# Halving the 512-column float32r products of a linear-attention and feed-forward layer, with their order and their weights' addresses changed

## The chip, the cores and the metric

The kernel runs on one core of a Trainium2 chip. The metric is device time in microseconds of one launch, as the median of several runs. Five engines matter: TensorE (PE in the profile; its weight loads are PEld), VectorE (DVE), ScalarE (ACT), GpSimd (POOL) and SyncE (SP), which issues the loads and stores.

## What is computed

One layer on `x` of 4 x 2048 tokens with 256 features, all in float32: a linear attention in chunks of 32 tokens, a residual and a layer norm, then a gated feed-forward part of 768 hidden features whose weights are integers, a residual and a layer norm. Cut to what matters:

```python
Q, K, V = x @ W_q.T, x @ W_k.T, x @ W_v.T
S = einsum('bncd,bnkd->bnck', Qc, Kc) * mask          # chunks of 32, causal, decayed
O = einsum('bnck,bnkd->bncd', S, Vc).reshape(B, T, D)
attn = sigmoid(x @ W_g.T) * O @ W_o.T + x
x = layernorm(x + attn)
h = silu(x @ (w_gate * SCALE).T) * (x @ (w_up * SCALE).T)
x = layernorm(x + h @ (w_down * SCALE).T)
```

## The kernel before

The 8192 tokens are cut into 16 blocks of 512 (`TB`), with features or tokens on the 128 partitions. The code is written out block by block in Python, so each engine's instructions follow in the order of the program text: `in_turn` keeps an instruction in that order, and nearly all of them are kept so. Each engine then works through its own queue and waits there for what the next instruction needs. A steady block of the trace mixes the stages of three token blocks: the feed-forward part of block b, the out projection of block n = b + 2, and the y, v and gate products of block m = b + 3.

Precision is kept by splitting operands. A float32 operand of the attention projections is split into a high and a low float32r part, and a third one called gap; a product then consists of three: high, low, and gap. `pieces_of_tokens` (L464) makes the parts of the tokens: `high` on ACT (x_hi, go_hi, L472), `low` on POOL (L476), `difference` on DVE (x_gap, go_gap, L481). `three` (L535) makes the products: for each of two PSUM banks the high and low products on TensorE and then a scaling of the bank in place on ACT (L542); its returned function `others` adds the gap products and then calls `finish` for each bank. `feature_major` (L495) has the weights of the layer as stationary operand and 512 columns of tokens moving: y (p_y) and the gate (p_g), L501. `token_major` (L513) has the tokens stationary and 256 columns moving: v (p_v) and the out projection (p_o), L523.

The feed-forward part splits into a float32r high and a float16 low part instead. `ffn_up` (L912) makes one of six hidden chunks hc: two high and two low products into the gate's bank (fg), as many into the up bank (fu), 512 columns each (L923), the high ones ahead for an even hc and the low ones for an odd one, then silu on ACT (s, L932). Its `multiply` makes u on DVE (L943), u_hi on ACT (L948) and u_lo on POOL (L949), at once or, when held, where the caller asks for it. `project_back_late` (L755) multiplies u with the down weights (fdn, L764, 256 columns): `high` and then `low`. `ffn_down` (L966) adds the residual on DVE (L982) and its moments.

The loop from L1157 sets the order. A steady block (b of at least 1, m below 16) issues: normalization of h on ACT, up 0, up 1, transposes of h on DVE (`move_h`, L867), y, the rest of up 1, up 2, y's third products with the yT copies on DVE (L567), up 3, scores (ps, L663), values (po, L699) and goT on DVE (L718), up 4, the parts of goT, v, gate, v's third products with two copies of v on ACT (L576), the gate's third with two tanh on ACT (L559), x_hi of the first half, up 5, x_hi of the second half and x_gap of the first, u of chunk 5, x_gap of the second half, out (`split_out`, L824), `split_h` (hT_hi on ACT, hT_lo on POOL, L899 and L900), the first two fdn chunks, out's third products, with the residual h on DVE (L832) and its moments, x_lo on POOL, the root on ACT, the other fdn chunks, high and then low, with minus_h, scale_h and shift_h on DVE (L388, L389) ahead of the ffn residual. Blocks with b of 1 to 11 cut the tokens of a later block (m + 1 below 16); b = 12 does not. The last two blocks have an order of their own.

PSUM has eight banks, taken in turn by `bank` (L118): a bank is free again when what was in it eight requests ago has been read. The tiles that live through the whole kernel, all weights and their parts among them, lie in one pool, `const`.

The function that a float32r product of 512 columns comes from, and the start of the steady order after the values:

```python
def feature_major(a, b):
    def product(i, pb, kind):
        for k in range(KD):
            in_turn(nc.tensor.matmul(pb, lhsT=a[kind][:, k, i * P : (i + 1) * P],
                                     rhs=b[kind][:, k, :], start=kind + k == 0,
                                     stop=True, skip_group_check=True))
    return product
```

Of the kernel before, what the change touches and what calls it, by code (L numbers as in the profile page):

```python
# [47 lines left out]
F32 = mybir.dt.float32  # L48
# [6 lines left out]
P = 128  # L55
# [21 lines left out]
def kernel(  # L77
# [21 lines left out]
    assert NB > 3  # L99

    const = ctx.enter_context(tc.tile_pool(name="const", bufs=1))
    setup = ctx.enter_context(tc.tile_pool(name="setup", bufs=2))
    xin = ctx.enter_context(tc.tile_pool(name="xin", bufs=2))
    work = ctx.enter_context(tc.tile_pool(name="work", bufs=2))
# [9 lines left out]

    def in_turn(ins):
        tc.keep_in_program_order(ins)

    def bank(name):  # L118
        return psum.tile([P, TB], F32, tag="ps", name=name)
# [22 lines left out]

    def load_w(eng, w, name, pieces=1):
        k, n = w.shape[0] // P, w.shape[1]
        t = const.tile([P, k, n], w.dtype, tag=name, name=name)
        per = k // pieces
        for i in range(0, k, per):
            eng.dma_start(
                t[:, i : i + per, :], w.rearrange("(k p) n -> p k n", p=P)[:, i : i + per, :]
            )  # L150
        return t
# [58 lines left out]
    nc.vector.memset(half, -0.5)  # L210


    m_sb = const.tile([P, KD, D], F32, tag="m", name="m_sb")

    def make_m():
        pm = bank("pm")
# [12 lines left out]

    diff = const.tile([P, CHUNK], I32, tag="diff", name="diff")
    for g in range(P // CHUNK):
        nc.gpsimd.iota(
            diff[g * CHUNK : (g + 1) * CHUNK, :],
# [1 line left out]
            base=0,  # L237
            channel_multiplier=-1,
        )
    chunk_mask = const.tile([P, CHUNK], F32, tag="chunk_mask", name="chunk_mask")  # L240
    nc.vector.tensor_scalar(chunk_mask, diff, 0.0, None, ALU.is_ge)
    table = tiny.tile([P, 1], F32, tag="table", name="table")
    in_turn(nc.scalar.activation(table, eps, AF.Sigmoid))
# [32 lines left out]
    def integers(w, w_int, name):  # L276

        k, n = w.shape[0] // P, w.shape[1]
        both = [
            const.tile([P, k, n], dtype, tag=f"{name}_{kind}", name=f"{name}_{kind}")  # L280
            for kind, dtype in (("hi", F32R), ("lo", F16))
        ]
# [20 lines left out]

    def wide_counter():

        wide = const.tile([P, top.shape[1]], F32, tag="wide", name="wide")
# [135 lines left out]
    def weight_parts(w, name, tags):  # L442

        hi, lo = (
            const.tile([P, KD, D], F32R, tag=tag, name=f"{name}_{kind}")
            for tag, kind in zip(tags, ("hi", "lo"))
        )
# [9 lines left out]
    def weight_gap(name):  # L457

        hi, lo = w_parts[name]
        gap = const.tile([P, KD, D], F32R, tag=name, name=f"{name}_gap")  # L460
# [27 lines left out]
    def token_parts(t, name):  # L488
# [3 lines left out]
            low(k)  # L492
        return parts, lambda: [difference(k) for k in range(KD)]

    def feature_major(a, b):  # L495


        def product(i, pb, kind):
            for k in range(KD):
                in_turn(  # L500
                    nc.tensor.matmul(  # L501
                        pb,
                        lhsT=a[kind][:, k, i * P : (i + 1) * P],
                        rhs=b[kind][:, k, :],
                        start=kind + k == 0,
                        stop=True,
                        skip_group_check=True,
                    )
                )

        return product

# [396 lines left out]
        while late_splits:  # L909
            late_splits.pop(0)()  # L910

    def ffn_up(b, hT, uT, chunks, cols=slice(0, TB), held=False, low_first=False):  # L912

        n = cols.stop - cols.start
        for hc in chunks:
            pg = bank(f"fg_{b}_{hc}_{cols.start}")[:, :n]
            pu = bank(f"fu_{b}_{hc}_{cols.start}")[:, :n]

            kinds = (1, 0) if hc % 2 or low_first else (0, 1)
            for kind in kinds:  # L920
                for pb, w in ((pg, fg), (pu, fu)):
                    for dc in range(KD):
                        product = nc.tensor.matmul(  # L923
                            pb,
                            lhsT=w[kind][:, dc, hc * P : (hc + 1) * P],
                            rhs=hT[kind][:, dc, cols],
                            start=(kind == kinds[0] and dc == 0),
                            stop=(kind == kinds[1] and dc == KD - 1),
                        )
                        in_turn(product)  # L930
            s = work.tile([P, n], F32, tag="s", name=f"s_{b}_{hc}")
            in_turn(nc.scalar.activation(s, pg, AF.Silu, scale=SCALE / H_UP))  # L932
# [7 lines left out]
            def multiply(hc=hc, pu=pu, s=s):  # L940
                u = work.tile([P, n], F32, tag="u", bufs=3, name=f"u_{b}_{hc}")
                in_steady_turn(
                    nc.vector.scalar_tensor_tensor(u, pu, U_UP / H_UP, s, ALU.mult, ALU.mult)  # L943
                )
                hi, lo = uT[0][hc][:, cols], uT[1][hc][:, cols]

                def split():
                    in_steady_turn(nc.scalar.copy(hi, u))  # L948
                    in_steady_turn(nc.gpsimd.tensor_tensor(lo, u, hi.bitcast(F32), ALU.subtract))  # L949

                if lagging:
                    late_splits.append(split)
                else:
                    split()

            if held:
                return multiply
            multiply()
# [198 lines left out]
    for b in range(NB - 2):  # L1157
# [8 lines left out]
        sT, v, sg = ahead  # L1166
        if not more:
            scales_next = iterated_scale_and_shift(mv_out, of_out, f"out_{b}")
        if b:
            normalize(hs[b + 1], *scales_h)  # L1170
            up_now(b, hT, uT, 0)
        multiply = ffn_up(b, hT, uT, range(1, 2), held=True)
        if b:
            moving = move_h(b + 1, hs[b + 1])
        else:
# [19 lines left out]
            moving = move_h(b + 1, hs[b + 1])  # L1195
        if not more:
            go_parts, go_gaps = token_parts(goT, f"go_{n}")
        multiply = ffn_up(b, hT, uT, range(3, 4), held=True)
        if b > 1:
            normalize(r_before, *scales_out, range(NG // 2, NG))  # L1200
        multiply()
# [2 lines left out]
        if more:  # L1204
            sT_next = attn_scores(m, yT)
            goT = attn_values(n, sT, v, sg)
            multiply = ffn_up(b, hT, uT, range(4, 5), held=True, low_first=True)
            go_parts, go_gaps = token_parts(goT, f"go_{n}")
            if b == 0:
                cast_fd(1, range(1))  # L1210
            multiply()
            go_gaps()
            v_next, v_rest = split_v(m, x_parts)
            sg_next, g_rest = split_gate(m, x_parts)
            v_rest()
            late = b > 0
            if late:
                g_rest()
                if m + 1 < NB:
                    x_parts, x_high, x_low, x_difference = pieces_of_tokens(  # L1220
                        xTs[m + 1], f"x_{m + 1}"
                    )
                    x_high(0)
                multiply = ffn_up(b, hT, uT, range(5, 6), held=True)
                if m + 1 < NB:
                    x_high(1)
                    x_difference(0)
                multiply()
                if m + 1 < NB:
                    x_difference(1)  # L1230
            else:
                if b == 0:
                    cast_fd(1, range(1, 2))
                up_with_cast(b, hT, uT, 5, 1, range(2, 3))
        else:
            up_now(b, hT, uT, 4)
# [349 lines left out]
    with tc.If(wide_any > 0, preferred_fallthrough_block=False):  # L1586
# [15 lines left out]
                nc.vector.tensor_scalar(t, t.bitcast(I32), SCALE, None, ALU.mult)  # L1602
                weights[-1].append(t)
        for name, (hi, lo, _) in w_parts.items():
            given[name] = const.tile([P, KD, D], F32, tag=name, name=f"{name}_whole")
# [47 lines left out]
```

## Time and profile before

| | |
|---|---|
| median of 3 runs | 485.84 us (485.81 to 486.66) |
| the profiled execution | 486.48 us, span 484.8 us |
| granted TensorE clock | 0.999 |
| TensorE busy, matmuls | 478.5 us (99%), 4760 |
| TensorE weight loads | 378.6 us (78%), 4760 |
| DVE busy | 348.9 us (72%), 795 |
| ACT busy | 370.8 us (76%), 699 |
| POOL busy | 281.5 us (58%), 285 |
| one steady block | 29.07 us |

The span reaches from the first to the last instruction of the profiled execution; busy times are of that one execution. Matmul durations in the rows contain the way through the array, which overlaps the next one, so the pace of TensorE is read from the distances of starts. A row of the timeline gives start, length, engine, line, operation, tiles written and read, shapes and count; what stands in brackets is idle time of the engine ahead of the row and what ended it. A block's length was read from windows cut at the start of the third out products.

### The profile page before, as it was taken

Reading aid. Unit: us, or ns where it says so; the run is one execution under the profiler, and the core shown is the slowest. Engines: PE = TensorE matmul, PEld = TensorE weight load, DVE = VectorE, ACT = ScalarE, POOL = GpSimd, SP = SyncE. Lnnn points to the kernel's source line nnn. Section 1 sums busy time; section 2 is a strip of 40 time slices with the busy share of each in tenths; the row PEclk is TensorE's granted clock in tenths of the full one; section 3 lists DMA queues with packets and bytes.
Section 4 is the critical chain, followed back from the end, with each engine's and each line's share of the span. In section 5 each row is a group of like instructions: output and inputs, shape, how many; then the busy total and the mean of one; then the engine's idle time right before and its main releaser. Section 6 shows DMA issues by size and latency. Waiting matters only on the chain.

```text
span 484.8 us, 12280 instructions
## 1 busy us (share of the span) xinstructions
PE 478.5 (99%) x4760; PEld 378.6 (78%) x4760; DVE 348.9 (72%) x795; ACT 370.8 (76%) x699; POOL 281.5 (58%) x285
## 2 busy tenths in 40 slices
PE   9999999999999999999999999999999999999995
PEld 5788787787868878687787868878687787868685
DVE  4587958777677776858777677876858777577656
ACT  4778788687888788797887888788797877786845
POOL 2835755655655566455655654566455655657764
PEclk9999999999999999999999999999999999999999
DMA  8630321211313114031321313114031211103102
GB/s 258 233 96 26 112 64 46 71 62 34 105 51 119 44 41 137 25 107 49 93 79 33 108 52 117 45 45 131 26 108 50 83 45 35 56 19 114 35 16 83
DMA packets 43323, 36.99 MB, mean 76 GB/s; under 512 B 4864, under 2 KB 39168, under 8 KB 43264
## 3 DMA queue, kind: packets, MB, share of 16 engines
q1 hardware_dynamic: 42144, 35.28, 23.6%
q10 hardware_dynamic: 1120, 0.92, 0.6%
q8 instruction: 38, 0.62, 0.5%
q14 instruction: 21, 0.17, 0.1%
HBM read 20.45 MB, written 8.39 MB: 59 GB/s over the span
## 4 chain that ended last, share of the span: by engine, by line
PE 98%; DMA 1%; DVE 0%; ACT 0%; issue 0%
PE fg L923 18%; PE fu L923 18%; PE fdn L764 13%; PE p_v L523 9%; PE p_y L501 9%; PE p_o L523 9%; PE p_g L501 9%; PE po L699 4%; PE ps L663 2%; PE fdn L1001 2%; PE fdn L1395 1%; PE fdn L745 1%; PE pg L587 1%; PE pa L811 1%; PE pv L629 1%; DMA wg<-in_w_gT_dram 1%
## 5 line engine op out<-in xcount | busy, mean ns | idle before, releaser
L949 POOL TENSOR_TENSOR u_lo<-u,u_hi 128x512 f16<-128x512 f32 (+1 forms) x98 | 129.6, 1329 | 92.7 <-ACT u_hi L948 92.7
L943 DVE SCALAR_TENSOR_TENSOR u<-fu,s 128x512 f32<-128x512 f32 (+1 forms) x98 | 66.1, 675 | 46.8 <-ACT s L932 44.8
L932 ACT ACTIVATE s<-fg 128x512 f32<-128x512 f32 (+1 forms) x98 | 57.5, 587 | 34.2 <-PE fg L923 33.3
L948 ACT CAST u_hi<-u 128x512 fp32r<-128x512 f32 (+1 forms) x98 | 59.5, 607 | 31.2 <-DVE u L943 31.2
L923 PE MATMUL fg<-hT_hi,fg_hi 128*128 128x512 f32 (+1 forms) x196 | 73.1, 454 | 0.0
L923 PE MATMUL fu<-hT_hi,fu_hi 128*128 128x512 f32 (+1 forms) x196 | 60.3, 389 | 0.0
L923 PE MATMUL fg<-hT_lo,fg_lo 128*128 128x512 f16 (+1 forms) x196 | 58.2, 379 | 0.0
L923 PE MATMUL fu<-hT_lo,fu_lo 128*128 128x512 f16 (+1 forms) x196 | 57.4, 375 | 0.0
L476 POOL TENSOR_TENSOR go_lo<-goT,go_hi 128x512 fp32r<-128x512 f32 x30 | 44.6, 1506 | 18.5 <-ACT go_hi L472 18.5
L481 DVE SCALAR_TENSOR_TENSOR go_gap<-go_hi,goT 128x512 fp32r<-128x512 f32 x30 | 48.3, 1647 | 0.8 <-ACT go_hi L472 0.7
L476 POOL TENSOR_TENSOR x_lo<-xT,x_hi 128x512 fp32r<-128x512 f32 x30 | 37.6, 1273 | 15.2 <-ACT x_hi L472 15.2
L923 PEld LDWEIGHTS fg<-hT_hi,fg_hi 128*128 128x128 f32 x196 | 35.6, 190 | 10.3
L923 PEld LDWEIGHTS fu<-hT_hi,fu_hi 128*128 128x128 f32 x196 | 36.5, 188 | 8.2
L481 DVE SCALAR_TENSOR_TENSOR x_gap<-x_hi,xT 128x512 fp32r<-128x512 f32 x30 | 21.9, 740 | 27.2 <-ACT x_hi L472 27.2
L900 POOL TENSOR_TENSOR hT_lo<-hT,hT_hi 128x512 f16<-128x512 f32 x28 | 35.7, 1295 | 4.6 <-ACT hT_hi L899 4.6
L832 DVE TENSOR_TENSOR h<-p_o,x 128x512 f32<-128x512 f32 x30 | 19.3, 685 | 25.3 <-PE p_o L523 23.2
L764 PE MATMUL fdn<-fd_hi,u_hi 128*128 128x256 f32 x288 | 36.5, 276 | 0.0
L923 PEld LDWEIGHTS <-fu_lo 128*128 128x128 f16 x196 | 19.2, 98 | 22.1
L764 PEld LDWEIGHTS fdn<-fd_hi,u_hi 128*128 128x128 f32 x288 | 34.4, 188 | 0.0
L764 PE MATMUL fdn<-fd_lo,u_lo 128*128 128x256 f16 x288 | 33.5, 273 | 0.0
L923 PEld LDWEIGHTS <-fg_lo 128*128 128x128 f16 x196 | 13.2, 98 | 21.8 <-issue 16.1
L764 PEld LDWEIGHTS <-u_lo 128*128 128x128 f16 x288 | 27.2, 98 | 3.4
(179 smaller groups left out, 1065.7 us busy)
## 6 DMA issues: line engine op xcount, KB each, us to landing
x<-in_x_dram SPq DMA_DIRECT2D x16, 512.0 KB, 3.8
xT<-in_xT_dram SPq DMA_DIRECT2D x15, 512.0 KB, 4.3
hT<-sq SPq DMA_DIRECT2D x224, 32.0 KB, 1.9
out_dram<-r SPq DMA_DIRECT2D x13, 512.0 KB, 3.3
out_dram<-r SPq DMA_DIRECT2D x7, 128.0 KB, 1.7
fg_int<-in_ffn_gT_dram SPq DMA_DIRECT2D x3, 256.0 KB, 7.3
fu_int<-in_ffn_uT_dram SPq DMA_DIRECT2D x3, 256.0 KB, 6.4
fd_int<-in_ffn_dT_dram SPq DMA_DIRECT2D x3, 256.0 KB, 5.5
```

What stands on the lines that cost most here:

```text
L476: in_turn(nc.gpsimd.tensor_tensor(lo[:, k, :], t[:, k, :], whole, ALU.subtract))
L481: nc.vector.scalar_tensor_tensor(gap[:, k, :], whole, -WHOLE, t[:, k, :], ALU.mult, ALU.add)
L501: nc.tensor.matmul(pb, lhsT=a[kind][:, k, i * P : (i + 1) * P], rhs=b[kind][:, k, :], start=kind + k == 0, stop=True, skip_group_check=True,)
L523: nc.tensor.matmul(pb[:, j * D : (j + 1) * D], lhsT=b[kind][:, k, g * P : (g + 1) * P], rhs=a[kind][:, k, :], start=kind + k + j == 0, sto ...
L699: product = nc.tensor.matmul(po[dims, dc * len(groups) + g, :], lhsT=v[rows, g, dc * P + dims.start : dc * P + dims.stop], rhs=sT[rows, g, :],
L764: nc.tensor.matmul(banks[g // per][:, g % per * D : (g % per + 1) * D], lhsT=part[:, g * P : (g + 1) * P], rhs=w, start=first and g % per ...
L900: nc.gpsimd.tensor_tensor(in_order[1], whole, in_order[0].bitcast(F32), ALU.subtract)
L923: product = nc.tensor.matmul(pb, lhsT=w[kind][:, dc, hc * P : (hc + 1) * P], rhs=hT[kind][:, dc, cols], start=(kind == kinds[0] and dc == ...
L932: in_turn(nc.scalar.activation(s, pg, AF.Silu, scale=SCALE / H_UP))
L943: nc.vector.scalar_tensor_tensor(u, pu, U_UP / H_UP, s, ALU.mult, ALU.mult)
L948: in_steady_turn(nc.scalar.copy(hi, u))
L949: in_steady_turn(nc.gpsimd.tensor_tensor(lo, u, hi.bitcast(F32), ALU.subtract))
```

## The change

It has four parts.

1. Every float32r product of 512 columns (`feature_major`, and the high products of the up chunks) becomes two of 256 columns with the same weights, into the two halves of the same bank.
2. `ffn_up` is cut into pieces: `ffn_pieces` returns the high products, the low products, and silu with the multiply, so that a caller can place each.
3. In the blocks with b of 1 to 12 the order of the pieces changes: the low (float16) products of up 0 and 1 come together ahead of their high ones, those of up 4 and 5 likewise, and up 2 and up 3 have the high products first. The high products of up 5 now stand between the gate's third products and v's third products; the gate comes ahead of v. On ACT, the copies of v and both x_hi come behind silu 5 and ahead of u_hi of chunk 5.
4. Three more pools shift where tiles lie: `steps` holds diff, `apart` holds chunk_mask and wide, and `still` holds the weights of the feature-major products (fg, fu, gate, m). Their addresses become 64 modulo 256 bytes, as the change states. No instruction is added by it.

```diff
+    steps = ctx.enter_context(tc.tile_pool(name="steps", bufs=1))
+    still = ctx.enter_context(tc.tile_pool(name="still", bufs=1))
+    apart = ctx.enter_context(tc.tile_pool(name="apart", bufs=1))
...
+    def home(tag):
+        return still if tag[:2] in ("fg", "fu", "wg") or tag in ("m", "wq", "wk") else const
...
+    def halves(cols):
+        return [slice(i, i + HB) for i in range(cols.start, cols.stop, HB)]
+
     def feature_major(a, b):
         def product(i, pb, kind):
             for k in range(KD):
-                in_turn(
-                    nc.tensor.matmul(
-                        pb,
-                        lhsT=a[kind][:, k, i * P : (i + 1) * P],
-                        rhs=b[kind][:, k, :],
-                        start=kind + k == 0,
+                for half in halves(slice(0, TB)):
+                    in_turn(
+                        nc.tensor.matmul(
+                            pb[:, half],
+                            lhsT=a[kind][:, k, i * P : (i + 1) * P],
+                            rhs=b[kind][:, k, half],
+                            start=kind + k + half.start == 0,
...
+    def ffn_pieces(b, hT, uT, hc, cols=slice(0, TB)):
+        pg = bank(f"fg_{b}_{hc}_{cols.start}")[:, :n]
+        pu = bank(f"fu_{b}_{hc}_{cols.start}")[:, :n]
+        fresh = [pg, pu]
+        def products(kind):
+            for i, (pb, w) in enumerate(((pg, fg), (pu, fu))):
+                for dc in range(KD):
+                    for part in [cols] if kind else halves(cols):
+                        product = nc.tensor.matmul(
+                            pb[:, part.start - cols.start : part.stop - cols.start],
+                            lhsT=w[kind][:, dc, hc * P : (hc + 1) * P],
+                            rhs=hT[kind][:, dc, part],
+                            start=len(fresh) > 1 - i,
...
+        return lambda: products(0), lambda: products(1), activate
...
+        late = more and b > 0
...
+        if late:
+            (high_0, low_0, silu_0), (high_1, low_1, silu_1) = pieces(0), pieces(1)
+            low_0()
+            low_1()
+            high_0()
+            silu_0()()
+            high_1()
+            multiply = silu_1()
...
-        multiply = ffn_up(b, hT, uT, range(3, 4), held=True)
+        multiply = ffn_up(b, hT, uT, range(3, 4), held=True, low_first=not late)
...
             if late:
+                (high_4, low_4, silu_4), (high_5, low_5, silu_5) = pieces(4), pieces(5)
+                low_4()
+                low_5()
+                go_parts, go_gaps = token_parts(goT, f"go_{n}")
+                high_4()
+                silu_4()()
+                go_gaps()
+                sg_next, g_rest = split_gate(m, x_parts)
+                v_next, v_rest = split_v(m, x_parts)
                 g_rest()
+                high_5()
+                multiply = silu_5()
+                v_rest()
                 if m + 1 < NB:
                     x_parts, x_high, x_low, x_difference = pieces_of_tokens(
                         xTs[m + 1], f"x_{m + 1}"
                     )
-                    x_high(0)
-                multiply = ffn_up(b, hT, uT, range(5, 6), held=True)
-                if m + 1 < NB:
-                    x_high(1)
+                    for k in range(KD):
+                        x_high(k)
                     x_difference(0)
                 multiply()
                 if m + 1 < NB:
                     x_difference(1)
```

In the diff's last part, `go_parts`, the cut of v and the gate, and up 4 stood ahead of the lines with a minus sign before the change, in the order given in the section on the kernel.

More of the change, by code (lines that the diff above doesn't have):

```diff
@@ L144, in load_w @@
         k, n = w.shape[0] // P, w.shape[1]
-        t = const.tile([P, k, n], w.dtype, tag=name, name=name)
+        t = home(name).tile([P, k, n], w.dtype, tag=name, name=name)
         per = k // pieces
@@ L210 @@
     nc.vector.memset(half, -0.5)
-    m_sb = const.tile([P, KD, D], F32, tag="m", name="m_sb")
+    m_sb = home("m").tile([P, KD, D], F32, tag="m", name="m_sb")
     def make_m():
@@ L228, in make_m @@
         in_turn(nc.scalar.copy(m_sb.rearrange("p k n -> p (k n)"), pm))
-    diff = const.tile([P, CHUNK], I32, tag="diff", name="diff")
+    diff = steps.tile([P, CHUNK], I32, tag="diff", name="diff")
     for g in range(P // CHUNK):
@@ L239 @@
         )
-    chunk_mask = const.tile([P, CHUNK], F32, tag="chunk_mask", name="chunk_mask")
+    chunk_mask = apart.tile([P, CHUNK], F32, tag="chunk_mask", name="chunk_mask")
     nc.vector.tensor_scalar(chunk_mask, diff, 0.0, None, ALU.is_ge)
@@ L279, in integers @@
         both = [
-            const.tile([P, k, n], dtype, tag=f"{name}_{kind}", name=f"{name}_{kind}")
+            home(name).tile([P, k, n], dtype, tag=f"{name}_{kind}", name=f"{name}_{kind}")
             for kind, dtype in (("hi", F32R), ("lo", F16))
@@ L304, in wide_counter @@
     def wide_counter():
-        wide = const.tile([P, top.shape[1]], F32, tag="wide", name="wide")
+        wide = apart.tile([P, top.shape[1]], F32, tag="wide", name="wide")
         in_turn(nc.vector.tensor_scalar(wide, top, EXACT, None, ALU.is_gt))
@@ L444, in weight_parts @@
         hi, lo = (
-            const.tile([P, KD, D], F32R, tag=tag, name=f"{name}_{kind}")
+            home(tag).tile([P, KD, D], F32R, tag=tag, name=f"{name}_{kind}")
             for tag, kind in zip(tags, ("hi", "lo"))
@@ L459, in weight_gap @@
         hi, lo = w_parts[name]
-        gap = const.tile([P, KD, D], F32R, tag=name, name=f"{name}_gap")
+        gap = home(name).tile([P, KD, D], F32R, tag=name, name=f"{name}_gap")
         in_turn(nc.gpsimd.tensor_tensor(gap, hi.bitcast(F32), lo.bitcast(F32), ALU.subtract))
@@ L499, in product @@
             for k in range(KD):
-                in_turn(
-                    nc.tensor.matmul(
-                        pb,
-                        lhsT=a[kind][:, k, i * P : (i + 1) * P],
-                        rhs=b[kind][:, k, :],
-                        start=kind + k == 0,
-                        stop=True,
-                        skip_group_check=True,
+                for half in halves(slice(0, TB)):
[5 more added lines that the diff above has]
+                            start=kind + k + half.start == 0,
+                            stop=True,
+                            skip_group_check=True,
+                        )
                     )
-                )
         return product
@@ L910, in no_more_splits, with activate @@
             late_splits.pop(0)()
-    def ffn_up(b, hT, uT, chunks, cols=slice(0, TB), held=False, low_first=False):
+    def ffn_pieces(b, hT, uT, hc, cols=slice(0, TB)):
         n = cols.stop - cols.start
[L915 to L922, printed above, removed]
+        pg = bank(f"fg_{b}_{hc}_{cols.start}")[:, :n]
[5 more added lines that the diff above has]
+                    for part in [cols] if kind else halves(cols):
                         product = nc.tensor.matmul(
-                            pb,
+                            pb[:, part.start - cols.start : part.stop - cols.start],
                             lhsT=w[kind][:, dc, hc * P : (hc + 1) * P],
-                            rhs=hT[kind][:, dc, cols],
-                            start=(kind == kinds[0] and dc == 0),
-                            stop=(kind == kinds[1] and dc == KD - 1),
+                            rhs=hT[kind][:, dc, part],
+                            start=len(fresh) > 1 - i,
+                            stop=True,
+                            skip_group_check=True,
                         )
                         in_turn(product)
+                        if len(fresh) > 1 - i:
+                            fresh.pop()
+        def activate():
             s = work.tile([P, n], F32, tag="s", name=f"s_{b}_{hc}")
@@ L938, in ffn_up, with multiply @@
                     )
-            def multiply(hc=hc, pu=pu, s=s):
+            def multiply():
                 u = work.tile([P, n], F32, tag="u", bufs=3, name=f"u_{b}_{hc}")
@@ L954, in multiply, with ffn_up @@
                     split()
+            return multiply
+        return lambda: products(0), lambda: products(1), activate
+    def ffn_up(b, hT, uT, chunks, cols=slice(0, TB), held=False, low_first=None):
+        for hc in chunks:
+            high, low, activate = ffn_pieces(b, hT, uT, hc, cols)
+            for products in (low, high) if (hc % 2 if low_first is None else low_first) else (high, low):
+                products()
+            multiply = activate()
             if held:
@@ L1168, with pieces @@
             scales_next = iterated_scale_and_shift(mv_out, of_out, f"out_{b}")
+        late = more and b > 0
+        def pieces(hc):
+            return ffn_pieces(b, hT, uT, hc)
         if b:
             normalize(hs[b + 1], *scales_h)
-            up_now(b, hT, uT, 0)
-        multiply = ffn_up(b, hT, uT, range(1, 2), held=True)
+        if late:
[6 more added lines that the diff above has]
+            multiply = silu_1()
+        else:
+            if b:
+                up_now(b, hT, uT, 0)
+            multiply = ffn_up(b, hT, uT, range(1, 2), held=True)
         if b:
@@ L1206 @@
             goT = attn_values(n, sT, v, sg)
[L1207 to L1216, printed above, removed]
-            if late:
+            if late:
+                (high_4, low_4, silu_4), (high_5, low_5, silu_5) = pieces(4), pieces(5)
[7 more added lines that the diff above has]
+                v_next, v_rest = split_v(m, x_parts)
                 g_rest()
+                high_5()
+                multiply = silu_5()
+                v_rest()
                 if m + 1 < NB:
@@ L1231 @@
             else:
-                if b == 0:
-                    cast_fd(1, range(1, 2))
+                multiply = ffn_up(b, hT, uT, range(4, 5), held=True, low_first=True)
+                go_parts, go_gaps = token_parts(goT, f"go_{n}")
+                cast_fd(1, range(1))
+                multiply()
+                go_gaps()
+                v_next, v_rest = split_v(m, x_parts)
+                sg_next, g_rest = split_gate(m, x_parts)
+                v_rest()
+                cast_fd(1, range(1, 2))
                 up_with_cast(b, hT, uT, 5, 1, range(2, 3))
@@ L1604 @@
         for name, (hi, lo, _) in w_parts.items():
-            given[name] = const.tile([P, KD, D], F32, tag=name, name=f"{name}_whole")
+            given[name] = home(name).tile([P, KD, D], F32, tag=name, name=f"{name}_whole")
             nc.vector.scalar_tensor_tensor(
```

## Prediction

> **What bounds the kernel now.** I read the page's busy shares first (TensorE 99%, DVE 72%, ACT 76%, POOL 58% of the span), then its chain of waits, shares by engine:
>
> ```profile
> PE 98%; DMA 1%; DVE 0%; ACT 0%; issue 0%
> ```
>
> TensorE is never out of work, and the chain that ended last is 98% TensorE. That alone would make every nanosecond of a product worth its face value, and would make the other engines free. A share is an average, though, so I next took one steady block (windows one block long: 29.07 us each, again and again, ACT busy 22.96 us and DVE 21.49 us of it) and asked how close the other engines run to TensorE where the change moves them. First TensorE, in order of time, from the scores of one block to the out projection's third product (start, length, what; the distance of two starts is the pace):
>
> ```profile
> 232.16 0.76 PE L663 MATMUL ps<-yT,xT 128*32 128x32 f32 x64
> 232.85 1.16 PE L699 MATMUL po<-sT,v 64*64 64x64 f32 x64
> 233.95 0.61 PE L923 MATMUL fg<-hT_lo,fg_lo 128*128 128x512 f16 x2
> ...
> 237.59 0.62 PE L501 MATMUL p_g<-x_hi,wg_hi 128*128 128x512 f32 x2
> ...
> 239.43 1.09 PE L523 MATMUL p_v<-wv_gap,x_gap 128*128 128x256 f32 x8
> ...
> 242.61 0.62 PE L923 MATMUL fu<-hT_hi,fu_hi 128*128 128x512 f32 x2
> ...
> 244.91 1.07 PE L764 MATMUL fdn<-fd_hi,u_hi 128*128 128x256 f32 x8
> 245.82 1.07 PE L523 MATMUL p_o<-wo_gap,go_gap 128*128 128x256 f32 x8
> 246.73 1.98 PE L764 MATMUL fdn<-fd_hi,u_hi 128*128 128x256 f32 x16
> ```
>
> The reader is to see paces. From 237.59 to 239.43 are 8 gate products of 512 columns: 230 ns each. From 246.73 to the next row of that timeline (248.54) are 16 of 256 columns, each with a weight load of its own: 113 ns each. Now ScalarE in the same stretch:
>
> ```profile
> 240.15 1.08 ACT L576 COPY v<-p_v 128x512 f32<-128x512 f32 x2
> 241.12 1.10 ACT L559 ACTIVATE sg<-p_g 128x512 f32<-128x512 f32 x2
> 242.08 0.65 ACT L472 ACTIVATE x_hi<-xT 128x512 fp32r<-128x512 f32 x1
> 242.81 0.60 ACT L932 ACTIVATE s<-fg 128x512 f32<-128x512 f32 x1
> 243.31 0.62 ACT L472 ACTIVATE x_hi<-xT 128x512 fp32r<-128x512 f32 x1
> 244.22 0.62 ACT L948 CAST u_hi<-u 128x512 fp32r<-128x512 f32 x1 [0.29 <-DVE u L943]
> 244.75 1.06 ACT L542 ACTIVATE p_o<-p_o 128x512 f32<-128x512 f32 x2
> 245.74 1.13 ACT L899 CAST hT_hi<-hT 128x512 fp32r<-128x512 f32 x2
> ```
>
> The two p_o rows are the in-place scalings (line 542) that the third out product needs. The first ends near 245.33, the second at 245.81; TensorE asks for their banks at 245.82 and 246.27. The slack is 0.5 us, and ScalarE works without a pause from the last x_hi on, except 0.29 us in which it waits for DVE's u. Last, what hangs on the third out product, one row of DVE and one of POOL:
>
> ```profile
> 250.54 0.92 DVE L388 TENSOR_SCALAR minus_h<-rstd_h 128x4 f32<-128x4 f32 x1
> ```
>
> ```profile
> 248.94 2.49 POOL L476 TENSOR_TENSOR x_lo<-xT,x_hi 128x512 fp32r<-128x512 f32 x2
> ```
>
> On DVE the residual h starts at 246.54 (after p_o), then moments, minus_h, the ffn residual, u, four transposes, u, u, and two yT copies follow nearly without a hole to 261.02, and the next block's scores start at 261.23. So a second loop, almost as long as TensorE's, runs through the block: scores, (TensorE) p_o, (DVE) next scores. TensorE's part from 245.82 to 261.23 is 15.41 us, and DVE's covers the same time with some 0.1 us to spare. Also, minus_h lasts 0.92 us and ends as POOL's second x_lo ends (251.46 and 251.43). In the last of these blocks, which has no x_lo, it lasts 0.17 us.
>
> **The change part by part.** *Halves.* A block has 48 float32r products of 512 columns (24 up, 12 y, 12 gate). Two halves at 113 ns are 226 to 227 against 230: -3.5 ns each, -0.17 us a block. The Trainium skill's page "TensorE: Matmul & The Clock Gate", section "Back-to-back issue gap", speaks against it: a gap is N/2.4 plus 2.5 ns, so two halves pay the constant twice, +2.5 ns a product, +0.12 us a block. Its figure for a whole product (216) is what the float16 rows show (223.05, 223.49, 223.92: 217 each), but not the 230 of the float32r rows; the row decides. The extra 48 weight loads are hidden if a load of the same weights behaves like a load of others, as in the 113 ns rows. If they never settled they would cost what the first halves after another shape cost (about 117 to 123): +0.2 to +0.9 us a block.
>
> *Weight addresses.* Nothing in the trace separates addresses: the same x_hi weights go at 117 at the beginning of a run and at 113 later. Bounds: 0, or 4 ns on each of 168 half products, -0.7 us a block, if they reach the 109 ns of float16. I take 0.
>
> *Three long runs.* Six float32r runs a block become three. A run's start costs some 8 ns for the switch and 25 ns for the first five halves, its end 10 ns: -0.13 us a block. With settled 256-column products elsewhere (-0.08), TensorE's own work falls by 0.3 to 0.4 us a block, half of it between scores and p_o, half behind it. The half behind it is worth at most 0.1 us, since DVE's loop is next.
>
> *What is moved.* The order of TensorE's work in the second half becomes scores, values, low 4, low 5, high 4, gate, v, gate's third, high 5, v's third, out. This moves v's third products from four places ahead of out to directly ahead of it, and ScalarE's order follows: v copies now stand behind silu 5, and **both** x_hi behind those, then u_hi, then the p_o scalings. Before, the v copies and one x_hi were done before silu 5. No DMA is moved past another queue's work here. Worked out from the scores at 232.16:
> - TensorE to the end of v's third product in its first bank: scores and values 1.79 (rows), low 4 and low 5 8 x 217 ns = 1.74, high 4 0.95 (8 x 113 and a run's start), gate 1.82, v 1.83, gate's third 0.91, high 5 0.91, half of v's third 0.45; sum 10.40, so 242.56. A finished bank is seen by ScalarE 0.20 us later (fg complete 242.61, s at 242.81).
> - ScalarE: v copies at 242.76 and 243.25, x_hi at 243.73, ready at 244.38. Starts are 0.49 apart when it is busy. The second x_hi goes at 244.2.
> - DVE in order: x_gap of the first half, 244.42, then u. Today they stand 0.73 apart, so u ends at 245.84.
> - ScalarE: u_hi 245.87, p_o scaling 246.40 to 246.98, the other to 247.46: today's times plus 1.65.
> - TensorE, unhindered, is through out and two fdn chunks at 245.75. It waits **1.3 us** for the first scaling. The fifth fu bank, too, is now released only by u at 245.84, and the second fdn bank needs it at 245.2, but that lies inside the same wait.
>
> Behind the wait are queued fdn and the next block's up products; who waits is DVE's residual, +1.2 us. On POOL the two hT_lo and two x_lo come with hT_hi, +1.65: the second x_lo ends near 253.1, and minus_h or the shift after it, reached at 251.7, waits for that. So the ffn residual moves by 1.2 (if it slips between) to 1.65. The front half of the next block has the same DVE and ScalarE order as today, so scores come as much later. A block grows by 1.2 to 1.65 us; I take 1.5, nearer the upper end, since the minus_h row shows that wait in all eleven blocks with x_lo. It applies to the 11 blocks that cut a later block's x (b from 1 to 11). In the twelfth there is no x_hi between, u_hi goes at 243.7, and nothing waits.
>
> *The rest.* First block, prologue and tail get only halves: some 140 products and a few runs, with waits among them, -0.5; block 12 -0.3. New homes of the weights move no instruction. Sum: 11 x 1.5 - 0.8 = +15.7 us. The profiled execution took 486.48 (span 484.8 and 1.7 around it), the median is 485.84, 0.1% off; from the median, **501.5 us**.
>
> **The rivals.**
> - *The wait is there, but DVE takes up the POOL part* (x_lo and minus_h do not collide): 11 x 1.15 - 0.8 = +11.9, 497.7. For it: minus_h may fall between the two x_lo. Against: then shift_h meets the second (in block 0, minus_h got through at an x_lo's end and shift_h lasted 1.2 us).
> - *TensorE sets the time, and the runs pay* (the faster side): 0.3 to 0.4 us in 12 blocks, capped behind p_o by DVE, and 0.5 outside: -3.3, 482.5. For it: the 98% chain. It decides if u_hi's chain is 1.3 us shorter than I count, that is if the p_o scalings end by 245.8; then the address of the weights may add up to -3.
> - *The second load of the same weights isn't hidden*: halves at 120 ns, +0.3 us a block between scores and p_o, on top of the wait: 505. Against: 113 ns rows with a load each.
> - *The change doesn't do what it says*: addresses are indifferent and a long run is no faster. That alone is -0.1 us a block and is hidden by the wait: 502.
>
> **How the numbers follow.** Wait with POOL's part 0.55, wait without it 0.22, with unhidden loads or indifferent addresses 0.08: slower together 0.85. TensorE's gain 0.12, and 0.03 for both cancelling. A measurement of this kernel tells 0.2% (1 us) from no change. The range goes from 494.5 (a wait of 1.0 with the best pace: 11 x 0.9 - 1) to 505; it leaves out the faster case and the worst loads.
>
> **What would show it.** Right: block length of 30.2 to 30.7 us in windows; TensorE idle about 1.3 us ahead of the third p_o products with releaser ACT p_o L542, eleven times, and again some 0.4 us ahead of ps with releaser DVE yT; ScalarE in the order v, v, x_hi, x_hi, u_hi, p_o, p_o; half products 113 ns apart. Wrong: no idle in TensorE and blocks under 29 us, or p_o scalings that end before out and two chunks of fdn are through; halves at 120 ns would make the slow case worse, at 109 ns would take 0.25 us a block from it.

## The result, and the profile after

The changed kernel takes 502.95 us (502.5 to 503.5, six runs) against 485.97 us (485.38 to 486.66, six runs): a ratio of 1.0349, with a 95% interval of 1.0336 to 1.0363. The forecast was 501.5, in a range of 494.5 to 505. The profiled execution took 502.74 us, with a span of 501.1; the granted clock is 0.999 as before, so the clock has no part in it.

The chain that ended last, from the page, by engine:

```profile
PE 89%; ACT 5%; DVE 3%; issue 1%; ACTq 0%
```

It was 98% TensorE. Now it leaves TensorE and goes through ScalarE and DVE. The windows of one steady block, from one start of the third out products to the next, before and after (columns: stretch, length, busy us and instructions of TensorE, weight loads, DVE, ACT, POOL, then the clock and the DMA):

```profile
216.75:245.82 29.07, 29.07 (x299) 23.24 (x297) 21.49 (x47) 22.96 (x44) 16.73 (x16) 1.00 0.25 74
```

```profile
223.28:253.87 30.59, 29.55 (x344) 26.12 (x344) 21.40 (x47) 23.13 (x44) 16.22 (x16) 1.00 0.24 71
```

A block has grown by 1.52 us. TensorE, which was never idle, now lacks work for 1.04 us of it. The 45 products more that the profile counts are the halves (48 in the program; a few records are missing in such a trace). Eleven such blocks make 16.7 of the 17.0 us. The hole stands in one place, eleven times (columns: total us, times, longest us):

```profile
PE p_o L535 <- ACT p_o L554: 11.4, 11, 1.0
```

TensorE's timeline after, from v's third products on:

```profile
249.03 1.09 PE L535 MATMUL p_v<-wv_gap,x_gap 128*128 128x256 f32 x8
...
251.77 1.07 PE L776 MATMUL fdn<-fd_hi,u_hi 128*128 128x256 f32 x8
253.87 1.23 PE L535 MATMUL p_o<-wo_gap,go_gap 128*128 128x256 f32 x8 [1.04 <-ACT p_o L554]
254.94 1.98 PE L776 MATMUL fdn<-fd_hi,u_hi 128*128 128x256 f32 x16
```

From 251.77 to 253.87 stand eight products that took 0.91 us before: a hole of 1.2 us. (The bracket says 1.04, since a row's length reaches past the start of the next.) What TensorE waits for is on ScalarE, and what ScalarE waits for is on DVE, whose own wait ends with ScalarE again:

```profile
249.12 0.60 ACT L949 ACTIVATE s<-fg 128x512 f32<-128x512 f32 x1
249.75 1.08 ACT L588 COPY v<-p_v 128x512 f32<-128x512 f32 x2
250.71 1.17 ACT L479 ACTIVATE x_hi<-xT 128x512 fp32r<-128x512 f32 x2
252.72 0.62 ACT L965 CAST u_hi<-u 128x512 fp32r<-128x512 f32 x1 [0.84 <-DVE u L960]
253.24 1.06 ACT L554 ACTIVATE p_o<-p_o 128x512 f32<-128x512 f32 x2
```

```profile
251.39 0.69 DVE L488 SCALAR_TENSOR_TENSOR x_gap<-x_hi,xT 128x512 fp32r<-128x512 f32 x1 [3.38 <-ACT x_hi L479]
252.00 0.68 DVE L960 SCALAR_TENSOR_TENSOR u<-fu,s 128x512 f32<-128x512 f32 x1
...
254.72 1.29 DVE L844 TENSOR_TENSOR h<-p_o,x 128x512 f32<-128x512 f32 x2 [1.44 <-PE p_o L535]
```

Read from the bottom: the first p_o scaling ends at 253.82, and TensorE starts at 253.87. The scaling stands behind u_hi (252.72), which waits for u on DVE (252.00 to 252.68). Silu 5 had been ready at 249.73, but u stands behind x_gap, x_gap behind the first x_hi (ready 251.36), and that behind two copies of v, which can't start before v's third products of the first bank are done (they start at 249.75). So a short work, u, that could have started at 249.8 started at 252.0.

The second thing to see is minus_h and POOL's x_lo:

```profile
258.72 1.20 DVE L395 TENSOR_SCALAR minus_h<-rstd_h 128x4 f32<-128x4 f32 x1
```

```profile
257.41 2.49 POOL L483 TENSOR_TENSOR x_lo<-xT,x_hi 128x512 fp32r<-128x512 f32 x2
```

minus_h has grown from 0.92 to 1.20 us and still ends as the second x_lo does (259.92 and 259.90), as the prediction had it. Whether TensorE's scores wait for it is another question, taken up in the account below.

### The profile page after: what moved, and what is told of

Read it like the earlier page. It is cut to its first block, busy times and chain, and to the rows that moved or that the text cites. A ratio compares the mean times of both kernels' runs of the same rounds, so it can differ in the third digit from the quotient of the medians.

```text
span 501.1 us, 13776 instructions
## 1 busy us (share of the span) xinstructions
PE 483.5 (96%) x5496; PEld 422.4 (84%) x5496; DVE 346.6 (69%) x795; ACT 372.1 (74%) x699; POOL 275.3 (55%) x285
## 4 chain that ended last, share of the span: by engine, by line
PE 89%; ACT 5%; DVE 3%; issue 1%; ACTq 0%
PE fg L935 18%; PE fu L935 17%; PE fdn L776 11%; PE p_y L513 9%; PE p_g L513 8%; PE p_v L535 7%; PE p_o L535 5%; PE po L711 4%; PE ps L675 2%; ACT v L588 2%; PE fdn L1029 2%; DVE x_gap L488 2%; DVE u L960 1%; ACT p_o L554 1%; ACT x_hi L479 1%
## 5 line engine op out<-in xcount | busy, mean ns | idle before, releaser
L935 PE MATMUL fg<-hT_hi,fg_hi 128*128 128x256 f32 x384 | 68.4, 300 | 0.0
L935 PE MATMUL fu<-hT_hi,fu_hi 128*128 128x256 f32 x384 | 61.0, 281 | 0.0
L935 PEld LDWEIGHTS fg<-hT_hi,fg_hi 128*128 128x128 f32 x384 | 54.8, 189 | 5.3
L935 PEld LDWEIGHTS fu<-hT_hi,fu_hi 128*128 128x128 f32 x384 | 52.1, 189 | 0.0
L483 POOL TENSOR_TENSOR go_lo<-goT,go_hi 128x512 fp32r<-128x512 f32 x30 | 39.2, 1326 | 14.4 <-ACT go_hi L479 14.4
L488 DVE SCALAR_TENSOR_TENSOR go_gap<-go_hi,goT 128x512 fp32r<-128x512 f32 x30 | 44.5, 1524 | 0.8 <-ACT go_hi L479 0.7
L479 ACT ACTIVATE go_hi<-goT 128x512 fp32r<-128x512 f32 x30 | 17.3, 624 | 22.4 <-DVE goT L730 22.4
```

The costliest lines, as they stand in the source:

```text
L479: in_turn(nc.scalar.mul(hi[:, k, :], t[:, k, :], TOP))
L483: in_turn(nc.gpsimd.tensor_tensor(lo[:, k, :], t[:, k, :], whole, ALU.subtract))
L488: nc.vector.scalar_tensor_tensor(gap[:, k, :], whole, -WHOLE, t[:, k, :], ALU.mult, ALU.add)
L935: product = nc.tensor.matmul(pb[:, part.start - cols.start : part.stop - cols.start], lhsT=w[kind][:, dc, hc * P : (hc + 1) * P], rhs=hT[k ...
```

## The experiments

All times are medians of four or five runs beside the kernel before on the same chip (485.98 to 486.14 us there). A block is the distance of two starts of the scores, or of the third out products, which is the same in the steady stretch. Paces and blocks are read from one profiled execution of each kernel. The diffs are shortened.

**Halves alone.** The order and the places of before; `feature_major` and the high up products in halves.

```diff
-                lhsT=a[kind][:, k, i*P:(i+1)*P], rhs=b[kind][:, k, :]
+                for half in halves(slice(0, TB)):
+                    lhsT=a[kind][:, k, i*P:(i+1)*P], rhs=b[kind][:, k, half]
```

> The order and the places of before, with every 512-column float32r product as two halves. The prediction's step (halves 113 ns, -0.17 us a block) gives some 483.5 us. What the trace of the changed kernel suggests instead, that halves with the same weights stand 118 ns apart and never settle, gives (235.5 - 229.5) ns x 48 = +0.29 us a block: about 490 us, and no wait of TensorE for p_o. If the halves carry the whole loss, it is about 503.

491.25 us, ratio 1.0100 (1.0084 to 1.0115); no wait for p_o; blocks of 29.43 us, +0.36. The halves cost instead of saving, but they are a third of the loss at most.

**Halves, with the weights moved.** The same, with the pools of the change.

> As the run with the halves alone, with the feature-major weights also in the pool of their own, at the changed addresses. If addresses are indifferent it has the same time as that run, within 0.3%, and the same pace of halves. If the addresses are what makes halves cheap, it is faster by up to 0.2 to 0.4 us a block, 3 to 5 us.

490.42 us, 1.0085 (1.0071 to 1.0099); blocks of 29.34. The traces differ by 0.09 us a block (the times, 0.8 us apart, overlap), and not because feature-major halves became cheap: y stays at 118 ns and the gate goes from 114 to 118, while fdn goes from 118 to 113 (the table is further down).

**The changed order with whole products.**

```diff
-        return [slice(i, i + HB) for i in range(cols.start, cols.stop, HB)]
+        return [cols]
```

> The changed kernel with whole 512-column products: its order and its addresses, no halves. The theory that ScalarE's new order makes the loss: the hole ahead of p_o's third products stays, 1.2 us or more in eleven blocks, and the time is 499.5 us if TensorE's saving counts in full, 501.5 if the loop through DVE to the next scores binds and eats half of it. The rival, that the halves make the loss, gives about 486.

502.49 us, 1.0346 (1.0332 to 1.0360); blocks mostly of 30.53. Taking the halves out of the changed kernel gives back almost nothing, and the moved places without the new order, in the run above, lose 4.3 us with the halves, so the order makes the loss. Whole products go in pairs of about 467 ns here, not the 457 of before, which fits that so little came back.

**x_hi early.** The changed kernel, with both x_hi behind v's scalings and x_gap behind u.

```diff
+                x_high(0), x_high(1)
                 g_rest()
                 high_5()
                 multiply = silu_5()
                 v_rest()
-                x_high(0), x_high(1)
-                x_difference(0)
                 multiply()
+                x_difference(0)
                 x_difference(1)
```

> The changed kernel with halves, but both x_hi on ScalarE directly behind v's scalings, ahead of the two tanh, and x_gap behind u of chunk 5. The theory of ScalarE's order: the first p_o scaling ends some 1.3 us earlier, TensorE does not wait for it, and a block takes 29.2 us if TensorE binds (488 us) or 29.5 if x_lo on POOL still holds minus_h (491 us). The rival, that the halves or the long runs make the loss: 500 to 503.

489.06 us, 1.0062 (1.0048 to 1.0076); blocks of 29.25. 13.9 of the 17.0 us are gone with no instruction added or left out. ScalarE's timeline of this kernel:

```profile
243.60 0.61 ACT L949 ACTIVATE s<-fg 128x512 f32<-128x512 f32 x1
244.07 1.09 ACT L588 COPY v<-p_v 128x512 f32<-128x512 f32 x2
245.02 0.67 ACT L965 CAST u_hi<-u 128x512 fp32r<-128x512 f32 x1
245.54 1.11 ACT L554 ACTIVATE p_o<-p_o 128x512 f32<-128x512 f32 x2
```

u_hi follows the copies without a pause, and the third out products start at 246.44, 0.91 us behind the start of the eight fdn products ahead of them, so with no hole:

```profile
245.53 1.07 PE L776 MATMUL fdn<-fd_hi,u_hi 128*128 128x256 f32 x8
246.44 1.07 PE L535 MATMUL p_o<-wo_gap,go_gap 128*128 128x256 f32 x8
```

**u ahead of x_gap.** One swap on DVE in the changed kernel, everything else as changed.

```diff
-                    x_difference(0)
                 multiply()
                 if m + 1 < NB:
+                    x_difference(0)
                     x_difference(1)
```

> The changed kernel with one swap on DVE alone: u of chunk 5 ahead of x_gap's first half; ScalarE's order, the halves and the long runs are as changed. Theory: u_hi comes late because u stands behind x_gap, which waits for x_hi, which stands behind the copies of v. Then u is ready 1.5 us earlier, u_hi follows the second x_hi directly, TensorE's wait falls from 1.3 to some 0.3 us, a block takes 29.6 us, and the time is 492 us. Rival, ScalarE's number of operations ahead of u_hi makes the wait: 500 to 503.

493.25 us, 1.0152 (1.0138 to 1.0166); blocks of 29.66. Its DVE, ScalarE and TensorE:

```profile
246.23 0.69 DVE L960 SCALAR_TENSOR_TENSOR u<-fu,s 128x512 f32<-128x512 f32 x1 [1.80 <-ACT s L949]
```

```profile
247.12 1.17 ACT L479 ACTIVATE x_hi<-xT 128x512 fp32r<-128x512 f32 x2
248.18 0.62 ACT L965 CAST u_hi<-u 128x512 fp32r<-128x512 f32 x1
248.69 1.08 ACT L554 ACTIVATE p_o<-p_o 128x512 f32<-128x512 f32 x2
```

```profile
248.17 1.07 PE L776 MATMUL fdn<-fd_hi,u_hi 128*128 128x256 f32 x8
249.34 1.23 PE L535 MATMUL p_o<-wo_gap,go_gap 128*128 128x256 f32 x8
```

u is done long before ScalarE comes to u_hi, and the hole shrinks to 0.26 us (1.17 between starts, less 0.91). So 9.7 us of the loss hang on the order of two DVE instructions; what is left of the hole goes with ScalarE's two x_hi ahead of u_hi, since the run with x_hi early has no hole.

**The second x_hi behind u_hi.**

```diff
-                    x_high(0), x_high(1)
+                    x_high(0)
                     x_difference(0)
                 multiply()
+                    x_high(1)
```

> The changed kernel with the second x_hi moved behind u_hi, x_gap's first half still ahead of u. By the prediction's wording (both x_hi stand ahead of u_hi) this takes one ScalarE operation, 0.49 us, out of the chain: 497.5 us. By the theory that the chain runs through x_gap and u on DVE, beside which the second x_hi lies hidden, nothing changes: 502 to 503 us.

509.86 us, 1.0498 (1.0483 to 1.0513): both expectations missed, in the same direction. ScalarE's timeline says why:

```profile
253.89 0.65 ACT L479 ACTIVATE x_hi<-xT 128x512 fp32r<-128x512 f32 x1
255.89 0.62 ACT L965 CAST u_hi<-u 128x512 fp32r<-128x512 f32 x1 [1.36 <-DVE u L960]
256.42 0.62 ACT L479 ACTIVATE x_hi<-xT 128x512 fp32r<-128x512 f32 x1
256.95 1.06 ACT L554 ACTIVATE p_o<-p_o 128x512 f32<-128x512 f32 x2
```

The second x_hi had lain in ScalarE's wait for u (0.84 us, now 1.36) and was free there. Behind u_hi it stands ahead of the p_o scalings, in the open: 0.53 us later in each of eleven blocks are 5.8 us, and 6.9 were measured. Part of the rest is that in five of these blocks the 16 fdn products behind the hole take 1.88 us instead of 1.82. The chain through x_gap and u is confirmed (the wait grew by what was taken out of it); the expectation had forgotten what stands behind u_hi.

**Whole products, with x_hi and x_lo early.** As x_hi early, with whole products again (`halves` returns `[cols]`) and with x_lo directly behind x_hi on POOL.

```diff
                     x_high(0), x_high(1)
+                    x_low(0), x_low(1)
```

> The run with x_hi early, with whole 512-column products, and with x_lo on POOL directly behind x_hi, so that minus_h meets no x_lo. If DVE's loop to the next scores bound there, the block falls by 0.3 us and more, to 485 us or below. If TensorE's own pace binds, minus_h gets short and the time hardly moves: only whole products against halves count, 466 against 471 ns a pair as in the run with the changed order and whole products, -0.1 us a block, 487.5 us.

487.95 us, 1.0047 (1.0033 to 1.0061). On DVE, minus_h is free of x_lo:

```profile
251.02 0.17 DVE L395 TENSOR_SCALAR minus_h<-rstd_h 128x4 f32<-128x4 f32 x1
```

Blocks take 29.17 at first and 29.34 later, beside 29.25 with minus_h at 1.14. Some 1 us of waiting per block was taken off DVE's loop in vain: the yT copies now end 0.44 us ahead of the scores (0.10 with x_hi early), and TensorE comes no earlier. In these two kernels TensorE's pace binds.

The step from 29.17 to 29.34 comes within this one execution. The same 16 fdn products, in an early block and in a late one:

```profile
188.86 1.98 PE L776 MATMUL fdn<-fd_hi,u_hi 128*128 128x256 f32 x16
190.67 2.79 PE L776 MATMUL fdn<-fd_lo,u_lo 128*128 128x256 f16 x24
```

```profile
335.27 2.05 PE L776 MATMUL fdn<-fd_hi,u_hi 128*128 128x256 f32 x16
337.16 2.79 PE L776 MATMUL fdn<-fd_lo,u_lo 128*128 128x256 f16 x24
```

They stand 113 ns apart in the first (1.81 us for 16) and 118 in the second (1.89), with out going the same way and v the other way (from 117.8 to 114.5), and it stays so to the end of the steady blocks.

**A pad of 128 bytes ahead of the feature-major weights**, in the kernel with x_hi early. It moves these weights and all tiles of the pools behind them.

```diff
+    pad = still.tile([P, 32], F32, tag="pad", name="pad")
+    nc.vector.memset(pad, 0.0)
```

> The run with x_hi early, with a tile of 128 bytes laid ahead of the feature-major weights, so that their addresses lie 128 bytes further. If the address of these weights sets the pace of the products (113 or 118 ns a half), runs of products change between the two paces and the time moves by up to 0.5 us a block, 3 to 6 us either way. If it is indifferent: 489 us, the same within 0.2%.

488.56 us, 1.0052 (1.0037 to 1.0066), blocks of 29.15. The sum hardly moved; the paces differ. The same y products, with x_hi early and with the pad (four halves a row):

```profile
226.16 0.64 PE L513 MATMUL p_y<-x_hi,m_hi 128*128 128x256 f32 x4
226.63 0.63 PE L513 MATMUL p_y<-x_lo,m_lo 128*128 128x256 f32 x4
227.10 0.63 PE L513 MATMUL p_y<-x_hi,m_hi 128*128 128x256 f32 x4
227.57 0.63 PE L513 MATMUL p_y<-x_lo,m_lo 128*128 128x256 f32 x4
```

```profile
226.55 0.62 PE L516 MATMUL p_y<-x_hi,m_hi 128*128 128x256 f32 x4
227.01 0.62 PE L516 MATMUL p_y<-x_lo,m_lo 128*128 128x256 f32 x4
227.46 0.62 PE L516 MATMUL p_y<-x_hi,m_hi 128*128 128x256 f32 x4
227.91 0.62 PE L516 MATMUL p_y<-x_lo,m_lo 128*128 128x256 f32 x4
```

0.47 us between starts without the pad, 0.453 with it: 118 against 113 ns a half.

**Three more places, and a pad in the kernel before.** Halves, long runs, x_hi and x_lo early, with 64 and with 192 bytes ahead of the weights, and with 128 bytes behind them; and the kernel before with 128 bytes between its weights and everything else.

> Halves, long runs, x_hi early on ScalarE and x_lo early on POOL, with 64 bytes laid ahead of the feature-major weights; these and all tiles of later pools lie 64 bytes further. If addresses choose between 113 and 118 ns for a whole run of products, the block lies anywhere from 28.8 us (all at 113; 484 us) to 29.4 us (all at 118; 491 us), and the shares of the two paces differ from those at 0 and at 128 bytes. If addresses are indifferent: 488.5 to 489 us with the same runs at 118 as without a pad.

> As the run with 64 bytes, with 192. The same two theories; by the one of the addresses this is the fourth of four places modulo 256, and one of the four may hold 113 ns in all three long runs: 484 us or less, under the time of before.

> As the run with 64 bytes, with 128 bytes laid behind the feature-major weights instead: the weights stay, tokens and activations move. If the place of the feature-major weights alone sets the pace, y, up and gate stay at 118 ns as in the run with x_hi early: 489 us. If the places of the tokens count, they change their pace: 486 to 488 us.

> The kernel before, its order and its whole products, with 128 bytes laid between the weights and everything else. If the kernel before owes its pace (457 ns for two whole products) to where its tiles lie, it gets slower by up to 0.2 to 0.3 us a block, 489 us; if not, 486 us.

491.89 us (1.0121, 1.0105 to 1.0137), 492.78 us (1.0141, 1.0125 to 1.0157), 492.83 us (1.0145, 1.0129 to 1.0161), and, for the padded kernel before, 488.47 us (1.0061, 1.0046 to 1.0075). The first three lie above all that was expected of them, and a pace of 120 ns was not foreseen. The mean distance from the start of a high product to the next one of its stage in nine steady blocks, in ns for 256 columns (a whole product counted as two; a run's slower start is in the mean):

| kernel | y (hi) | gate (hi) | v (hi) | out (hi) | fdn | us |
|---|---|---|---|---|---|---|
| before | 114.5 | 114.7 | 115.9 | 115.9 | 113.3 | 486 |
| before, 128 bytes behind the weights | 116.5 | 117.0 | 117.7 | 113.3 | 113.3 | 488.5 |
| halves alone | 117.8 | 114.0 | 115.1 | 117.3 | 117.6 | 491.3 |
| halves, weights moved | 117.7 | 117.6 | 117.8 | 115.8 | 113.3 | 490.4 |
| x_hi early | 117.8 | 117.8 | 115.7 | 113.3 | 113.3 | 489.1 |
| x_hi early, 128 bytes ahead | 113.3 | 113.3 | 113.5 | 117.8 | 117.8 | 488.6 |
| both early, 64 bytes ahead | 113.4 | 117.2 | 119.1 | 118.6 | 118.6 | 491.9 |
| both early, 192 bytes ahead | 113.3 | 117.8 | 120.0 | 120.0 | 120.0 | 492.8 |
| both early, 128 bytes behind | 117.7 | 117.3 | 117.4 | 117.7 | 117.8 | 492.8 |

None of the four places (0, 64, 128 and 192 bytes ahead) held 113 in all runs, and no version beats the kernel before.

## Why the prediction was right, point by point

- **ScalarE's order and the wait for p_o.** Right, in place, count (eleven) and cause. Counted from the scores (238.96 in the block shown), the first p_o scaling was to end at 14.82 us and ended at 14.86. On the way v's copies came 0.19 us later than reckoned, and u followed x_gap by 0.61 us, not by the 0.73 that I took from a pair in which u had waited for its silu. The hole is 1.2 us where 1.3 was reckoned, since TensorE itself came to it 0.13 us later (13.72 for 13.59). The prediction's words put the cause down to ScalarE's queue ("both x_hi behind those, then u_hi"), while its sum runs through x_gap and u on DVE. The swap on DVE showed that the sum had the path: the longer part is the crossing to DVE and back, and the second x_hi costs nothing where it stands.
- **What comes behind.** Wrong in mechanism. The prediction had the wait on POOL's x_lo add up to 0.4 us in scores that come late. minus_h did lengthen, but TensorE does not wait at the scores. Its last up products, the scores and DVE's yT copies ahead of them, in the changed kernel and in the one with whole products and both early:

```profile
238.43 0.59 PE L935 MATMUL fu<-hT_lo,fu_lo 128*128 128x512 f16 x2
238.96 0.76 PE L675 MATMUL ps<-yT,xT 128*32 128x32 f32 x64
237.62 1.27 DVE L579 COPY yT<-p_y 128x512 f32<-128x512 f32 x2
```

```profile
232.05 0.59 PE L935 MATMUL fu<-hT_lo,fu_lo 128*128 128x512 f16 x2
232.58 0.76 PE L675 MATMUL ps<-yT,xT 128*32 128x32 f32 x64
230.86 1.28 DVE L579 COPY yT<-p_y 128x512 f32<-128x512 f32 x2
```

The scores start 0.53 us behind the start of the up row in both, though the copies end 0.07 us ahead in the first and 0.44 in the second. The sign that the prediction named, 0.4 us ahead of ps with DVE's yT as the releaser, does stand in the trace, for weight loads, but the kernel before has it too (4.0 us in 11 waits), and so has the second kernel above (5.1 us in 12, as in the changed one): it tells nothing. The scores come at 15.68 us from the third out products against 15.41 before, and TensorE's own work accounts for about that: it restarts after the hole with a first distance of 223 instead of 113 ns and unsettled ones behind, and its products are slower. The copies are ready only 0.07 us before the scores, though; what a TensorE at the reckoned pace would have met there was not tried. Two readings ahead of this term were loose: DVE's loop has 1.31 us in which it waits for a silu of ScalarE (ahead of the u at 259.13), so it is not DVE's alone, and the copies of before end 0.21 us ahead of the scores (261.02 and 261.23), not 0.1.
- **Halves.** Wrong in sign: -0.17 us a block reckoned, +0.36 measured in the places of before and +0.27 in the new ones. The failing step is "113 ns are what a half costs", taken from products of 256 columns in another stage. The trace had 113 and 117 for the same weights, and I put 117 down to the beginning of a run. It is a second pace that a whole run can keep. The ends of my bound (117 to 123 ns, +0.2 to +0.9; by its own figures the upper end is 0.8) held the measured cost; the value I took was at the wrong end. The rival that a second load of the same weights isn't hidden does not hold in general: with the pad of 128 bytes such pairs of halves go at 113.3. The rule of the Trainium skill that I set aside (page "TensorE: Matmul & The Clock Gate", section "Back-to-back issue gap": N/2.4 plus 2.5 ns, so an estimated +0.12 us a block for the second constant) had the sign right, but not its size nor, as the table shows, its cause: the same halves run at 113 or 118. That section gives the rule for a single matmul, which the prediction left out, and about 131 ns for one of 512 columns in a stream; the streams here go at 217 (float16) and about 230 (float32r), so the measurement decides.
- **Addresses.** Taken as nothing, within a bound of -0.7 us. Paces do differ with the places (with a pad y and gate go at 113.3 instead of 117.8, v at 113.5 instead of 115.7, and out and fdn the other way), but in the change's own move and with that pad the sum over a block moved by 0.1 us only; in the kernel before, a pad costs 0.18 us a block and 2.4 us in all.
- **Long runs.** -0.21 us a block reckoned; -0.09 shown (29.34 with halves and moved weights in the old order, 29.25 with x_hi early). That they pay less fits that a long run can be long at the slow pace.
- **The sum.** 1.5 us a block were predicted and 1.52 measured, partly by compensation. Predicted were 1.2 for the wait, with a saving of TensorE taken off, and 0.3 for POOL's part. Measured are 1.2 for the hole, about 0.15 for TensorE's restart behind it, and 0.18 for halves and runs together (the block with x_hi early, 29.25, against 29.07 before). Outside the eleven blocks -0.8 us was reckoned and +0.3 measured. So by mechanism the kernel did what the rival of 497.7 us had, a wait whose POOL part TensorE does not pay, though x_lo and minus_h did collide; restart and slower products put back about what that left out. That the total is so close is luck; that the loss is the wait is shown by the two reorderings, which take 13.9 and 9.7 us off.

What stays open: why a run of float32r products settles at 113, 118 or 120 ns. The runs show that a pad can change the pace, and that the pace is often kept through a run and across stages with other tiles (out, once settled, fdn and out's third products mostly agree). Places can't be all of it, since the kernel with whole products and both early changes its paces in the middle of one execution. The runs do not show which tiles' places count, if any: padding ahead of the weights moves the tokens too; and the last three pads were put into a kernel in which x_lo is early as well, so that they differ from the other two in more than the pad.

## What to carry to other kernels

When TensorE is 100% busy, list for each wait that it just doesn't have by how much it doesn't: here 0.5 us of slack ahead of p_o were worth more than all that could be gained on its products. When an instruction is moved on one queue, follow the chain through every queue that it crosses: u waited behind x_gap on DVE, for x_hi on ScalarE, for a product on TensorE. And a filler that lies in an engine's wait is free only there; moved behind what the engine waited for, it costs its full time.

## What the runs showed of the hardware that was not expected

Float32r products of 256 columns, each with a weight load, have more than one steady pace: 113.3 ns, 117.8 ns and, with 192 bytes of padding, 120.0 ns; whole ones of 512 columns go in pairs of about 457 or 467. With one pad of 128 bytes y and gate went at 113 instead of 118 and out and fdn at 118 instead of 113; in another kernel out and fdn went from 113 to 118 within one execution. The kernel before lost 0.5% (488.47 against 486.11 us) when its tiles lay elsewhere, with the same instructions apart from one memset.
